# Two GRUs over a history on one Trainium2 core: sorted key rows written whole, sums moved to GpSimd, a count in bf16, results placed by one product

## The chip, the core and the metric

The kernel runs on one core of one Trainium2 chip. The metric is the device time of one launch in microseconds (us), as the median of several runs. Five engines work side by side: TensorE (PE, with its weight loads PEld), VectorE (DVE), ScalarE (ACT), GpSimd (POOL) and SyncE (SP), which here only issues DMA transfers. GpSimd issues the gathers (DMAs that fetch rows by a list of indices).

## The reference

A recommendation model (batch B = 1024, history of T = 100 steps, width H = 128). A GRU runs over the history and gives a key per step; an attention MLP scores each key against the item; the masked softmax of the scores pools the keys. The first 100 columns of the pooled array, transposed, are then the attention weights of a second recurrence (AUGRU) over the same keys. A final MLP reads the AUGRU's state at each row's own length.

```python
_, gru_seq = jax.lax.scan(gru_step, h0, jnp.swapaxes(item_historical_embedding, 0, 1))
keys = jnp.swapaxes(gru_seq, 0, 1)
feat = jnp.concatenate([keys, q, keys - q, q * keys], axis=-1)
score = _mlp(feat, [(att_W0, att_b0), (att_W1, att_b1), (att_W2, att_b2)], jax.nn.relu)
score = jnp.where(mask[:, :, None] == 1, score, -jnp.inf)
attn = jax.nn.softmax(score, axis=1)[..., 0]
pooled = jnp.einsum('bt,btd->bd', attn, keys)
att_seq = pooled.T[:T]
def augru_step(h, inp):
    x_t, a_t = inp
    ti = jnp.concatenate([h, x_t], axis=-1)
    r = jax.nn.sigmoid(ti @ aug_Wr.T + aug_br)
    u = jax.nn.sigmoid(ti @ aug_Wu.T + aug_bu)
    h_hat = jnp.tanh(jnp.concatenate([h * r, x_t], axis=-1) @ aug_Wh.T + aug_bh)
    u = a_t[:, None] * u
    h_new = (1.0 - u) * h + u * h_hat
    return (h_new, h_new)
...
attention_feature = jnp.take_along_axis(aug_out, sequential_length - 1, axis=1)
comb = jnp.concatenate([user_embedding, item_embedding, hist_sum, item_embedding * hist_sum, attention_feature], axis=1)
scores = _mlp(comb, [...], jax.nn.sigmoid)
```

`hist_sum` is the masked sum of the history divided by the length. The AUGRU needs a row only up to its length.

## The kernel before

The batch is two halves of 512 rows; the 128 hidden values lie on the partitions, the rows of a half along the free dimension. Instructions are written in the order in which each engine runs them (a manual schedule), so a transfer that waits on SP holds up every transfer written after it on SP, and likewise on each engine.

**First phase (`gru_phase`).** Steps s = 0 to 99 for both halves. PE multiplies (L588), ACT and DVE do the gates, the attention MLP of a step follows one step later (L770). Its scores, one row per half and step, go by a small DMA on SP into `s_b` (L825). After a group of steps DVE transposes `s_b` (L865), the softmax is carried on, and the pooled sums are updated with pairs of operations (L699 the product, L700 the sum, L689 the rescaling of the old sum), on GpSimd or DVE. Keys are collected in `kt` tiles, and every four steps `store` (L669) writes them to DRAM (`keys_d`) on SP, for later. Besides, a bf16 mask `m` is loaded per step and GpSimd sums the history (L573, L574). At step 8 a count of the rows still alive at each step (`count`, L354) is made on PE: a product of the 0/1 table `alive` with `ones`. It says which of three tables of widths the second phase may take (`over_d`).

**The tail of the first phase**, after the loop: attention of the last steps, the last softmax, the pooled sums of the remaining keys. The sums of the columns that are needed first (`soon`, 64 values a partition) come before those of the others (`rest`, 448 values). Of the first, `first_w` (L1114), PE's `by_row` and `first` and DVE's L1136 and L1137 make the AUGRU's first state `h_all`. Then the pooled array is written to DRAM (`pooled_d`, 8 DMAs on SP, L1146) and the last keys are stored (L669).

**Second phase (`augru_phase`).** Steps t = 1 to 99. The batch is sorted by length, so the width of a step shrinks (510, 506, 500, ...). `half_step` does one half: L1264 (the key's part of the three gates), L1268 (the state's part), ACT L1276, L1292, L1293, DVE L1298 to L1308. It needs the keys in sorted order, which indirect DMAs on POOL fetch from `keys_d` (`load_row`, L193); from step 12 on each is held back by a one-column copy (L192) from the product `rest` of L1308. PE and DVE transpose them (L1246, L1253). The attention weights are gathered from `pooled_d` into `att_r`, transposed (L1213), written to `att_d` and loaded to all partitions by SP as `at` (L1200, L1216, L1228), used in L1305. Late steps are done for both halves at once. Rows whose state is final go through the last MLP in blocks of 128 (`predict`); the very last block is placed by L1496 into the array of all results, which holds them 32 times over the partitions.

Keys are stored in groups. READ is the number of steps in a gathered group: 4, then 8 for each. So the keys of steps 4 to 11 are one group of `keys_d`, in 128 x 256 pieces, 32 gathers of 128 KB in all: 4 on POOL at the last GRU step but one, 4 behind the loop (L193), 8 behind the sums of half 0 and 16 in the second phase.

Of the kernel before, what the change touches and what calls it, by code (L numbers as in the profile page):

```python
# [9 lines left out]
F32 = mybir.dt.float32  # L10
# [42 lines left out]
WHOLE = 1  # L53
READ = [G] * WHOLE + [2 * G] * ((T - WHOLE * G) // (2 * G))
READ += [T - sum(READ)] * (sum(READ) < T)
# [30 lines left out]
def kernel(ctx: ExitStack, tc: tile.TileContext, a: dict, out: bass.AP):  # L86
# [31 lines left out]
        dram.tile([B, n * P] if q < WHOLE else [NK * P, n * R], F32, name=f"keys_d{q}")  # L118
        for q, n in enumerate(READ)
    ]  # L120
    mask_d = dram.tile([T, B], BF16, name="mask_d")
    inv_d = dram.tile([B, 3], I32, name="inv_d")
# [22 lines left out]
    used_s = const.tile([P, NH, GH, T - SOON], U8, name="used_s")  # L145
    all_y = pooled.rearrange("p k r -> p (k r)")[:, :BQ]
    idx_p = const.tile([P, HB // PR], I32, name="idx_p")
# [19 lines left out]
    def load_rows(q, i, width, tiles):  # L167

        n = READ[q]
        if q < WHOLE:  # L170
            r = rows[q, i] = tiles.tile([P, GH, n * P], F32, tag="once", name="rows")
            for g in range(GH):
                gather(r[:, g, :], keys_d[q], g, i)
                yield
            return

        parts, tag = (2, "kt") if tiles is kx else (1, "rows")
        some = [
            tiles.tile([P, KH // parts, n * R], F32, tag=tag, name="rows") for _ in range(parts)
        ]  # L180
        rows[q, i] = some
        for k in range(-(-width // R)):
            load_row(q, i, k)
            yield

    def load_row(q, i, k):
        some = rows[q, i]
        part, at = divmod(k, KH // len(some))
        r = some[part]
        if later.get("pace") is not None:  # L190

            nc.gpsimd.tensor_copy(r[:, at, 0:1], later["pace"])  # L192
        nc.gpsimd.indirect_dma_start(  # L193
            out=r[:, at, :],
            out_offset=None,
            in_=keys_d[q],
            in_offset=bass.IndirectOffsetOnAxis(ap=idx_k[:, k, i : i + 1], axis=0),
        )
# [5 lines left out]
    def gru_phase(pools):  # L204
# [72 lines left out]
        def load_later():  # L277
# [57 lines left out]

            alive = mid.tile([P, NG, T], F32, name="alive", **once)
            nc.vector.tensor_tensor(
# [4 lines left out]
            )  # L342
            ones = pre.tile([P, 1], F32, name="ones")
            nc.gpsimd.memset(ones, 1.0)
# [194 lines left out]
        class Half:  # L539
# [127 lines left out]
            def store(self, q):  # L667
                row, part = divmod(q - WHOLE, 2)
                nc.sync.dma_start(  # L669
                    out=keys_d[WHOLE + row].rearrange("(k p) m -> p k m", p=P)[  # L670
                        :, self.ks, ts(part, G * R)
                    ],
                    in_=self.kt[q].rearrange("p k n c -> p k (n c)"),
                )
# [256 lines left out]
        early = [load_rows(0, i, HB, mid) for i in range(NH)]  # L931
        more_early = load_rows(1, 0, HB, kx)

        def gather_early(n):
            for _ in range(n):
                next(more_early)


        late, again, early_from = 6, 24, 84
        for s in range(T):  # L940
# [5 lines left out]
            def loads():  # L946
# [6 lines left out]
                if s == T - AHEAD:  # L953
# [50 lines left out]
            if s == T - 2:  # L1004
                gather_early(4)
            for half in halves:
# [21 lines left out]

        gather_early(4)
        some(0, 1)  # L1030
# [31 lines left out]
        exponents()  # L1062
        take(T + 1)
        some(4, 5)

# [84 lines left out]
        halves[0].store(q)  # L1150
        all_of(more_early)

    def augru_phase(pools, widths, alive):
# [260 lines left out]
        def predict(g, last=False):  # L1414
# [22 lines left out]
            if last:  # L1437
                p0 = [of_pool("p0")[:MC, :P] for _ in range(n)]
                for j in range(n):
                    nc.tensor.matmul(  # L1440
                        p0[j], lhsT=part[:, ts(j, MC)], rhs=ident, start=True, stop=False
                    )
                yield
                for j in range(n):
# [39 lines left out]
            nc.scalar.activation(f1, p1, AF.Sigmoid, bias=later["c1"])  # L1484
            yield
            p2 = of_pool("p2")[:, 0:1]
# [3 lines left out]
            nc.scalar.activation(y, p2, AF.Sigmoid, bias=later["c2"])  # L1490
            if not last:
                rows_of(early_d, y, True, None)
                return
            p = of_pool("po")[:, :BQ]
            for q in range(P // R):
                nc.tensor.matmul(  # L1496
                    p[ts(q, R), :],
                    lhsT=y.to_broadcast([P, R]),
                    rhs=later["places"][q // 2][:, ts(q % 2, BQ)],
                    start=True,  # L1500
                    stop=True,
                )
            nc.vector.tensor_add(all_y, p, all_y)

        def last_places():
            own = sp.tile([P, 1], F32, name="own3", bufs=1)
            nc.gpsimd.tensor_copy(own, idx_p[:, 0:1])
            later["places"] = []
            for i in range(NH):
                row = wp.tile([P, HB], F32, tag="att_r", name="places", bufs=2)  # L1510
                nc.gpsimd.iota(
                    row,
                    pattern=[[1, HB]],
                    base=i * HB,
                    channel_multiplier=0,
                    allow_small_or_imprecise_dtypes=True,
                )
                nc.gpsimd.tensor_scalar(row, row, own, None, ALU.is_equal)
                later["places"].append(row)

        def earlier_results():
            nc.sync.dma_start(
                out=all_y,
                in_=early_d.rearrange("(q c) o -> q (o c)", c=BQ)
                .unsqueeze(1)
                .to_broadcast([P // R, R, BQ]),
            )
# [4 lines left out]

        def spread(q):


            ahead = 3 if widths[FIRST[q]] > HB // 2 else 4
            n = NH * -(-widths[FIRST[q]] // R)
            return spread_over(n, NH * (FIRST[q] - FIRST[q - 1] + 1 - ahead))

# [8 lines left out]
        sorted_rows = [gather_weights(i) for i in range(NH)]  # L1548
        ahead = load_rows(1, 1, widths[FIRST[1]], kp)
        for _ in range(P // R):  # L1550
            next(ahead)
        due = spread_over(-(-widths[FIRST[1]] // R) - P // R, NH * (FIRST[1] - 2))
        jobs, final = [], None
        for t in range(1, T):
            if t == one:
                open_state(t - 1, 1)
                last_state(1)
            if t + 1 in FIRST[1:-1]:
                all_of(ahead)
                ahead, due = gathers(FIRST.index(t + 1) + 1), spread(FIRST.index(t + 1) + 1)  # L1560
            for i in range(NH):
# [60 lines left out]
    with none.Else():  # L1622
# [8 lines left out]
        out=out.rearrange("(q c) -> q c", c=BQ),  # L1631
        in_=all_y.rearrange("(q r) c -> q r c", r=R)[:, 0, :],
    )
# [66 lines left out]
```

## Time and profile before

| what | us |
|---|---|
| median of 3 runs | 1998.83 (1998.15 to 1998.97) |
| the profiled execution | 2015.4 |
| its span, on which all rows stand | 2013.5 |
| mean granted clock of PE | 0.995 |

A row of a timeline reads: start in us, duration, engine, line, operation, output<-input, shape, count, and in brackets how long the engine stood idle before and what released it. A row of waits reads: engine, tile and line <- releaser: us in total, times, longest. A row of windows gives a stretch, its length, the busy time of each engine with its number of instructions, PE's granted clock, the DMA engines' share and GB/s.

### The profile page before, as it was taken

What the parts mean: (1) busy time and instruction counts of PE and PEld (TensorE: products, weight loads), DVE (VectorE), ACT (ScalarE), POOL (GpSimd) and SP (SyncE); (2) the same over time, 40 slices, a digit from 0 to 9 for tenths busy, and PEclk for the clock granted to TensorE, in tenths of its full rate; (3) what the DMA queues carried; (4) which work ended last, traced back from release to release, by engine and by line L of the source; (5) the groups of instructions that cost most, each with busy time, mean ns of one, the idle gap of its engine ahead of it and who ended that gap; (6) DMA issues with size and microseconds to landing.
All of it is one profiled execution on the core that took longest, in us unless ns stands there. A gap on an engine that the chain in (4) does not pass through costs nothing.

```text
span 2013.5 us, 40927 instructions
## 1 busy us (share of the span) xinstructions
PE 1982.8 (98%) x15324; PEld 875.7 (43%) x15324; DVE 1674.2 (83%) x3036; ACT 940.4 (47%) x1689; POOL 1262.1 (63%) x1300
## 2 busy tenths in 40 slices
PE   9999999999999999999999999999699999999998
PEld 2333333333333333333333333334244556678997
DVE  7888998887888897888888898998477777888885
ACT  4445444444445454445445454455234444445553
POOL 0333939569796959495987767989553354445331
PEclk9999999999999999999999999999899999999999
DMA  4443333323334334333432333332443333333331
GB/s 124 98 117 100 98 107 107 105 84 90 107 115 108 108 117 122 109 115 105 126 101 80 99 107 92 107 107 83 126 136 93 95 110 98 94 104 95 81 81 35
DMA packets 244572, 205.59 MB, mean 102 GB/s; under 512 B 61811, under 2 KB 207068, under 8 KB 244364
## 3 DMA queue, kind: packets, MB, share of 16 engines
q1 hardware_dynamic: 231852, 170.31, 29.9%
q0 software_dynamic: 12224, 32.05, 5.7%
q8 instruction: 122, 2.00, 0.4%
q14 instruction: 86, 0.70, 0.1%
q10 hardware_dynamic: 288, 0.52, 0.1%
HBM read 146.75 MB, written 54.42 MB: 100 GB/s over the span
## 4 chain that ended last, share of the span: by engine, by line
PE 93%; DVE 2%; POOL 2%; another core or an unknown queue 1%; ACT 1%; issue 1%; DMA 0%; SPq 0%; DVEq 0%; ACTq 0%; POOLq 0%
PE ps L588 48%; PE pm L770 17%; PE ph L1268 4%; PE pr L1268 4%; PE pu L1268 4%; PE ph L1264 4%; PE pr L1264 4%; PE pu L1264 4%; POOL pooled L700 1%; PE last L737 1%; POOL kw L699 1%; PE pr L1359 0%; PE ph L1359 0%; POOL hist L574 0%
## 5 line engine op out<-in xcount | busy, mean ns | idle before, releaser
L588 PE MATMUL ps<-x,wih 128*32 128x512 f32 x4800 | 601.9, 592 | 0.0
L588 PE MATMUL ps<-hn,whh 128*32 128x512 f32 x4752 | 596.8, 592 | 0.0
L588 PEld LDWEIGHTS ps<-x,wih 128*32 128x32 f32 x4800 | 174.4, 110 | 342.6 <-issue 337.9
L588 PEld LDWEIGHTS ps<-hn,whh 128*32 128x32 f32 x4752 | 172.8, 110 | 339.1 <-issue 337.0
L600 ACT ACTIVATE r<-ps,brz 128x512 f32<-128x512 f32 x200 | 137.5, 687 | 381.9 <-PE ps L588 381.7
L573 POOL TENSOR_TENSOR xm<-x,m 128x512 f32<-128x512 f32 x200 | 233.5, 1168 | 66.9 <-DMA m<-mask_d 66.6
L574 POOL TENSOR_TENSOR hist<-hist,xm 128x512 f32<-128x512 f32 x200 | 257.7, 1288 | 15.7
L193 POOL DMA_INDIRECT rows<-keys_d,idx_k x218 | 211.9, 972 | 85.2 <-POOL rows L192 49.7
L700 POOL TENSOR_TENSOR pooled<-pooled,kw 128x512 f32<-128x512 f32 x192 | 245.0, 1276 | 15.0
L699 POOL TENSOR_TENSOR kw<-kt,e 128x512 f32<-128x512 f32 x192 | 206.3, 1074 | 69.0 <-DVE e L888 69.0
L621 ACT ACTIVATE ps<-ps,bih 128x512 f32<-128x512 f32 x198 | 131.1, 662 | 229.8 <-DVE ps L618 228.7
L770 PE MATMUL pm<-hn,wk 128*32 128x512 f32 x1200 | 214.9, 592 | 0.0
L770 PE MATMUL pm<-kq,wkq 128*32 128x512 f32 x1200 | 214.8, 592 | 0.0
L1276 ACT ACTIVATE c<-ph,bh 128x510 f32<-128x510 f32 (+57 forms) x174 | 88.1, 506 | 254.5 <-PE ph L1268 222.1
L608 DVE SCALAR_TENSOR_TENSOR u<-ps,bhh,r 128x512 f32<-128x512 f32 x198 | 147.5, 745 | 68.8 <-PE ps L588 66.6
L770 PE MATMUL pm<-mv,w 128*32 128x512 f32 (+1 forms) x808 | 194.9, 592 | 1.0 <-DVE e L869 1.0
L192 POOL COPY rows<-rest 128x1 f32<-128x1 f32 x186 | 34.9, 188 | 209.5 <-DVE rest L1308 205.5
L631 DVE TENSOR_TENSOR d<-hn,ps 128x512 f32<-128x512 f32 x198 | 136.1, 687 | 35.9 <-ACT ps L621 35.5
L618 DVE TENSOR_TENSOR ps<-ps,u 128x512 f32<-128x512 f32 x200 | 140.0, 700 | 25.2 <-remote 4.1
L632 DVE TENSOR_TENSOR d<-ps,d 128x512 f32<-128x512 f32 x198 | 136.9, 691 | 26.1 <-ACT ps L622 11.1
L642 ACT COPY hn<-ps 128x512 f32<-128x512 f32 x198 | 115.5, 583 | 91.6 <-DVE kq L637 89.9
L1298 DVE TENSOR_TENSOR pu<-pu,c 128x510 f32<-128x510 f32 (+57 forms) x173 | 81.8, 473 | 89.7 <-ACT c L1276 62.9
(271 smaller groups left out, 3141.3 us busy)
## 6 DMA issues: line engine op xcount, KB each, us to landing
x<-in_hist_x SPq DMA_DIRECT2D x210, 256.0 KB
keys_d<-kt SPq DMA_DIRECT2D x48, 1024.0 KB
m<-mask_d SPq DMA_DIRECT2D x200, 128.0 KB
rows<-keys_d,idx_k POOLq DMA_INDIRECT x218
s_b<-mv SPq DMA_DIRECT2D x200, 8.0 KB
keys_d<-kt SPq DMA_DIRECT2D x32, 64.0 KB
mask_i<-in_mask SPq DMA_DIRECT2D x8, 200.0 KB
part_d<-part SPq DMA_DIRECT2D x2, 400.0 KB
```

The lines of the kernel that those rows point to most:

```text
L193: nc.gpsimd.indirect_dma_start(out=r[:, at, :], out_offset=None, in_=keys_d[q], in_offset=bass.IndirectOffsetOnAxis(ap=idx_k[:, k, i : i + ...
L573: nc.gpsimd.tensor_mul(d, x, m)
L574: nc.gpsimd.tensor_add(acc, acc, d)
L588: nc.tensor.matmul(p[ts(q, R), :], lhsT=w[:, g, ts(q, R)], rhs=v, start=(j == 0), stop=(j == len(parts) - 1),)
L600: nc.scalar.activation(r, pr, AF.Sigmoid, bias=brz[:, 0:1])
L608: nc.vector.scalar_tensor_tensor(out=u, in0=ph, scalar=bhh[:, 2:3], in1=r, op0=ALU.add, op1=ALU.mult,)
L618: nc.vector.tensor_add(pi, pi, u)
L699: eng.tensor_mul(d, k, w)
L700: eng.tensor_add(acc, acc, d)
L770: nc.tensor.matmul(p[i][s, :], lhsT=w[:, s], rhs=v, start=start, stop=stop)
L1264: nc.tensor.matmul(p, lhsT=m[:, 1, :], rhs=k, start=True, stop=False)
L1268: nc.tensor.matmul(p, lhsT=m[:, 0, :], rhs=v, start=False, stop=True)
```

## The change

1. Keys of steps 4 to 11 go to DRAM as whole rows (`wide_d`, one row of 1024 values per batch row: eight steps of 128). `sort_rows` gathers them whole (128 rows of 4 KB, 512 KB a gather, four a half) and stores them in sorted order (`sorted_d`, two stores of 1 MB a half, on SP). `load_sorted` loads from there, four plain DMAs of 256 KB a half on SP: steps 4 to 7 before the branch, steps 8 to 11 at step 3. The READ groups are 4, 4, 4, then 8 each. From step 12 on the gathers are as before.
2. The last sums of half 1 (`halves[1].pool(T, ..., rest)`) run on GpSimd instead of DVE.
3. `alive` and `ones` are bf16.
4. The last block of results is placed by one product: the final MLP's last product is added onto a 128 x 4 table that is 0 where a row belongs in a quarter of the batch and -1e30 elsewhere, so the sigmoid leaves 0 there; one product with `places` puts them on 4 rows of 256. The earlier results are loaded as 4 x 256 instead of broadcast, and written out from there.

```diff
-READ = [G] * WHOLE + [2 * G] * ((T - WHOLE * G) // (2 * G))
+READ = [G] * WIDE + [2 * G] * ((T - WIDE * G) // (2 * G))
...
+    wide_d = dram.tile([B, wide * P], F32, name="wide_d")
+    sorted_d = [dram.tile([HB, wide * P], F32, name=f"sorted_d{i}") for i in range(NH)]
...
+    def sort_rows(i):
+        pair = GH // 2
+        for part in range(GH // pair):
+            t = kx.tile([P, pair, wide * P], F32, tag="kt", name="sort")
+            for g in range(pair):
+                gather(t[:, g, :], wide_d, part * pair + g, i)
+            yield
+            nc.sync.dma_start(
+                out=sorted_d[i][ts(part, pair * P), :].rearrange("(g p) m -> p g m", p=P),
+                in_=t,
+            )
+    def load_sorted(q, i, tile):
+        n = READ[q] * R
+        rows[q, i] = [tile]
+        for p in range(P // R):
+            nc.sync.dma_start(
+                out=tile[ts(p, R)],
+                in_=sorted_d[i].rearrange("(k r) (p m) -> p r k m", r=R, p=P // R)[p][
+                    :, :, ts(q - WHOLE, n)
+                ],
+            )
...
-            alive = mid.tile([P, NG, T], F32, name="alive", **once)
+            alive = mid.tile([P, NG, T], BF16, name="alive", **once)
-            ones = pre.tile([P, 1], F32, name="ones")
+            ones = pre.tile([P, 1], BF16, name="ones")
...
             def store(self, q):
+                if q < WIDE:
+                    to = wide_d[self.cols, :].rearrange("(k r) (p m) -> p r k m", r=R, p=P // R)
+                    for p in range(P // R):
+                        nc.sync.dma_start(
+                            out=to[p][:, :, ts(q - WHOLE, G * R)],
+                            in_=self.kt[q][ts(p, R)].rearrange("p k n c -> p k (n c)"),
+                        )
+                    return
...
                 if last:
+                    all_of(sort[0])
...
             if s == T - 2:
-                gather_early(4)
+                next(sort[0])
+                next(sort[0])
...
-        gather_early(4)
+        next(sort[1])
+        next(sort[1])
         some(0, 1)
...
         take(T + 1)
+        all_of(sort[1])
...
         for half in halves:
-            half.pool(T, nc.vector, rest)
+            half.pool(T, nc.gpsimd, rest)
...
         halves[0].store(q)
-        all_of(more_early)
+        for half in halves:
+            load_sorted(WHOLE, half.i, kx.tile([P, KH, G * R], F32, tag="kt", name="rows"))
...
+            if last:
+                nc.tensor.matmul(p2, lhsT=f1, rhs=later["m2"].to_broadcast([M1, B // BQ]),
+                    start=False, stop=True)
+                y = sp.tile([P, B // BQ], F32, name="y4", bufs=1)
+                nc.scalar.activation(y, p2, AF.Sigmoid, bias=later["c2"])
+                p = of_pool("po")[: B // BQ, :BQ]
+                nc.tensor.matmul(p, lhsT=y, rhs=later["places"], start=True, stop=True)
+                nc.vector.tensor_add(all_y, p, all_y)
+                return
...
-            p = of_pool("po")[:, :BQ]
-            for q in range(P // R):
-                nc.tensor.matmul(p[ts(q, R), :], lhsT=y.to_broadcast([P, R]),
-                    rhs=later["places"][q // 2][:, ts(q % 2, BQ)], start=True, stop=True)
-            nc.vector.tensor_add(all_y, p, all_y)
...
-        ahead = load_rows(1, 1, widths[FIRST[1]], kp)
-        for _ in range(P // R):
-            next(ahead)
-        due = spread_over(-(-widths[FIRST[1]] // R) - P // R, NH * (FIRST[1] - 2))
+        ahead, due = iter(()), []
...
+            if t + 1 == FIRST[WHOLE]:
+                for i in range(NH):
+                    tile = kp.tile([P, KH, G * R], F32, tag="rows", name="rows")
+                    load_sorted(WHOLE + 1, i, tile)
```

**SP in the tail.** The rows from the score transfers of step 97 to those of step 100 (one pair of `s_b` per step; `sorted_d_73` is half 0, `sorted_d_74` half 1, `q` a small table), before and after:

```order
691 L825 DMA s_b_149<-mv 4x1x512
692 L825 DMA s_b_151<-mv 4x1x512
693 L962 DMA q_153<-perm_d 32x2x512
694 L825 DMA s_b_145<-mv 4x1x512
695 L825 DMA s_b_147<-mv 4x1x512
696 L825 DMA s_b_145<-mv 4x1x512
697 L825 DMA s_b_147<-mv 4x1x512
698 L825 DMA s_b_149<-mv 4x1x512
699 L825 DMA s_b_151<-mv 4x1x512
```

```order
691 L196 DMA sorted_d_73<-sort 128x2x1024
692 L860 DMA s_b_151<-mv 4x1x512
693 L860 DMA s_b_153<-mv 4x1x512
694 L196 DMA sorted_d_73<-sort 128x2x1024
695 L994 DMA q_155<-perm_d 32x2x512
696 L196 DMA sorted_d_74<-sort 128x2x1024
697 L860 DMA s_b_147<-mv 4x1x512
698 L860 DMA s_b_149<-mv 4x1x512
699 L860 DMA s_b_147<-mv 4x1x512
700 L860 DMA s_b_149<-mv 4x1x512
701 L860 DMA s_b_151<-mv 4x1x512
702 L860 DMA s_b_153<-mv 4x1x512
```

The score transfers of step 98 (the second pair) and 99 (the third) now stand behind three stores of sorted rows, the last of them half 1's first.

**SP at the handover**, from the pooled array's stores to the second attention load (`at`) of half 1, before and after:

```order
704 L669 DMA keys_d_72<-kt 128x16x128
705 L1146 DMA pooled_d<-pooled 32x16x32 x8
706 L669 DMA keys_d_72<-kt 128x16x128
707 L1620 UNCONDITIONAL_BRANCH
708 L1623 COMPARE_AND_BRANCH
709 L1200 DMA att_d_78<-att_t 4x512
710 L1228 DMA at<-att_d_78 128x506
711 L1228 DMA at<-att_d_78 128x500
712 L1200 DMA att_d_79<-att_t 4x512
```

```order
708 L704 DMA keys_d_71<-kt 128x16x128
709 L1181 DMA pooled_d<-pooled 32x16x32 x8
710 L704 DMA keys_d_71<-kt 128x16x128
711 L206 DMA rows<-sorted_d_73 32x16x128 x4
712 L206 DMA rows<-sorted_d_74 32x16x128 x4
713 L1673 UNCONDITIONAL_BRANCH
714 L1676 COMPARE_AND_BRANCH
715 L1236 DMA att_d_80<-att_t 4x512
716 L1264 DMA at<-att_d_80 128x506
717 L1264 DMA at<-att_d_80 128x500
718 L1236 DMA att_d_81<-att_t 4x512
719 L1264 DMA at<-att_d_81 128x506
```

Eight loads of sorted rows, four a half, now stand between the last key store and the first write of the attention weights.

**POOL at the handover**, from the last sums of half 0 to the first gathers of the attention weights (`att_r`), before and after:

```order
866 L689 TENSOR_TENSOR pooled<-pooled,e 128x16x28
867 L699 TENSOR_TENSOR kw<-kt,e 128x16x28
868 L700 TENSOR_TENSOR pooled<-pooled,kw 128x16x28
869 L699 TENSOR_TENSOR kw<-kt,e 128x16x28
870 L700 TENSOR_TENSOR pooled<-pooled,kw 128x16x28
871 L193 DMA rows<-keys_d_61,idx_k 128x256 x8
872 L1619 TENSOR_LOAD over_d
873 L1620 UNCONDITIONAL_BRANCH
874 L1623 COMPARE_AND_BRANCH
875 L1696 ISA
876 L158 DMA att_r<-pooled_d,idx 128x128
```

```order
869 L734 TENSOR_TENSOR kw<-kt,e 128x16x28
870 L735 TENSOR_TENSOR pooled<-pooled,kw 128x16x28
871 L734 TENSOR_TENSOR kw<-kt,e 128x16x28
872 L735 TENSOR_TENSOR pooled<-pooled,kw 128x16x28
873 L724 TENSOR_TENSOR pooled<-pooled,e 128x16x28
874 L734 TENSOR_TENSOR kw<-kt,e 128x16x28
875 L735 TENSOR_TENSOR pooled<-pooled,kw 128x16x28
876 L734 TENSOR_TENSOR kw<-kt,e 128x16x28
877 L735 TENSOR_TENSOR pooled<-pooled,kw 128x16x28
878 L1672 TENSOR_LOAD over_d
879 L1673 UNCONDITIONAL_BRANCH
880 L1676 COMPARE_AND_BRANCH
```

Eight gathers ahead of the branch are gone, and seven sums of half 1 stand there.

More of the change, by code (lines that the diff above doesn't have):

```diff
@@ L175, in load_rows @@
             return
[L177 to L181, printed above, removed]
+        rows[q, i] = [tiles.tile([P, KH, n * R], F32, tag="rows", name="rows")]
         for k in range(-(-width // R)):
@@ L184, in load_rows @@
             yield
+    def sort_rows(i):
[19 more added lines that the diff above has]
+            )
     def load_row(q, i, k):
-        some = rows[q, i]
-        part, at = divmod(k, KH // len(some))
-        r = some[part]
+        r = rows[q, i][0]
         if later.get("pace") is not None:
-            nc.gpsimd.tensor_copy(r[:, at, 0:1], later["pace"])
+            nc.gpsimd.tensor_copy(r[:, k, 0:1], later["pace"])
         nc.gpsimd.indirect_dma_start(
-            out=r[:, at, :],
+            out=r[:, k, :],
             out_offset=None,
@@ L931, in gru_phase @@
         early = [load_rows(0, i, HB, mid) for i in range(NH)]
[L932 to L936, printed above, removed]
+        sort = [sort_rows(i) for i in range(NH)]
         late, again, early_from = 6, 24, 84
@@ L1442, in predict @@
                     )
+                p2 = of_pool("p2")[:, : B // BQ]
+                nc.tensor.matmul(p2, lhsT=ident, rhs=later["others"], start=True, stop=False)
                 yield
@@ L1485, in predict @@
             yield
+            if last:
+                nc.tensor.matmul(
+                    p2,
+                    lhsT=f1,
+                    rhs=later["m2"].to_broadcast([M1, B // BQ]),
+                    start=False,
+                    stop=True,
+                )
+                y = sp.tile([P, B // BQ], F32, name="y4", bufs=1)
[4 more added lines that the diff above has]
+                return
             p2 = of_pool("p2")[:, 0:1]
@@ L1490, in predict @@
             nc.scalar.activation(y, p2, AF.Sigmoid, bias=later["c2"])
-            if not last:
-                rows_of(early_d, y, True, None)
-                return
-            p = of_pool("po")[:, :BQ]
-            for q in range(P // R):
[L1496 to L1503, printed above, removed]
+            rows_of(early_d, y, True, None)
         def last_places():
```

66 lines of the change are left out of this document (43 added, 23 removed).

## The prediction

> **What bounds the kernel now.** I read the page first (busy shares, then the chain that ended last), then windows over the joint between the two phases, then the timelines there.
>
> ```profile
> span 2013.5 us, 40927 instructions
> PE 1982.8 (98%) x15324; PEld 875.7 (43%) x15324; DVE 1674.2 (83%) x3036; ACT 940.4 (47%) x1689; POOL 1262.1 (63%) x1300
> PE 93%; DVE 2%; POOL 2%; another core or an unknown queue 1%; ACT 1%; issue 1%; DMA 0%; SPq 0%; DVEq 0%; ACTq 0%; POOLq 0%
> ```
>
> PE is busy 98% and carries 93% of the chain, so an edit counts only where PE stops. The change hardly touches the two long loops. It touches the start (a count), the joint near 1380 to 1455, and the last 4 us. Windows there (columns: us, then busy time and count of PE, PEld, DVE, ACT, POOL, then PE's granted clock, DMA share, GB/s):
>
> ```profile
> 1380.00:1405.00 25.00, 24.70 (x138) 14.37 (x138) 21.97 (x67) 18.67 (x35) 21.76 (x23) 1.00 0.33 100
> 1430.00:1453.00 23.00, 10.35 (x27) 4.55 (x25) 4.04 (x8) 2.73 (x5) 14.71 (x16) 0.75 0.38 113
> 1453.00:1470.00 17.00, 16.57 (x37) 7.67 (x38) 14.07 (x25) 6.60 (x10) 5.83 (x10) 0.84 0.42 112
> ```
>
> The second is the only real hole: PE busy 10.35 of 23 us, with POOL's 16 gathers in it, the very ones removed. Is it in the timed runs? DVE's, PE's and ACT's rows:
>
> ```profile
> 1432.11 0.69 DVE L1308 SCALAR_TENSOR_TENSOR rest<-pu,h_all 128x506 f32<-128x506 f32 x1
> 1454.82 0.69 DVE L1308 SCALAR_TENSOR_TENSOR rest<-pu,h_all 128x506 f32<-128x506 f32 x1
> 1470.89 0.68 DVE L1308 SCALAR_TENSOR_TENSOR rest<-pu,h_all 128x496 f32<-128x496 f32 x1
> 1475.94 0.68 DVE L1308 SCALAR_TENSOR_TENSOR rest<-pu,h_all 128x496 f32<-128x496 f32 x1
> 1436.46 1.00 PE L1264 MATMUL ph<-k,wh 128*128 128x500 f32 x2
> 1447.14 2.04 PE L1264 MATMUL pu<-k,wu 128*128 128x500 f32 x2 [9.68 <-issue]
> 1448.97 1.06 PE L1213 MATMUL pw<-ident,att_r 128*96 128x128 f32 x4
> ACT k L1247 <- remote: 12.0, 1, 12.0
> ```
>
> L1308 comes once per half step: 1432.11 is step 2 of half 0, 1470.89 step 4 of half 0, four half steps on, and the next comes 5.05 later. At that pace the fourth would stand at 1452.3, so the hole costs 18.6; up to two groups like L1213 (1.06 each) are extra work in it, so 16.5 to 18.6. The profiled execution took 2015.4 against a median of 1998.83: 16.6 longer. So nearly all the hole belongs to the profiled execution alone. That fits its look: ACT's wait has no releaser in this program ("remote"), and PE went on to 1437.5 before it stopped. I work against the profiled times but leave the hole out: of it the timed runs hold 0 to 18.6 − 16.6 = 2.0.
>
> **The change, part by part.**
>
> *A. The gathers of steps 4 to 11.* 32 gathers of 128 KB go, 8 of 512 KB and four 1 MB stores come. In timed runs this can only give back what is left of the hole: 0 to 2.0. I take the middle, **−1.0**. The extra store transfers at steps 8 and 12 sit in the GRU loop, on SP alone; I cost them at nothing, covered by inputs that are loaded steps ahead, and if that cover fails PE waits for a load there, within my upper bound.
>
> *B. The last sums of half 1.* Seven 448-wide DVE operations move behind GpSimd's own sums.
>
> ```profile
> 1409.00 0.69 DVE L1137 TENSOR_TENSOR h_all<-first,s_b 128x512 f32<-128x512 f32 x1
> 1409.61 0.62 DVE L699 TENSOR_TENSOR last<-kt,last 128x448 f32<-128x448 f32 x1
> 1413.43 0.62 DVE L700 TENSOR_TENSOR pooled<-pooled,last 128x448 f32<-128x448 f32 x1
> 1413.45 1.12 PE L1264 MATMUL ph<-hist,wh 128*128 128x510 f32 x2 [1.48 <-DVE last L699]
> 1405.07 0.97 POOL L699 TENSOR_TENSOR kw<-kt,e 128x448 f32<-128x448 f32 x1
> 1406.12 1.14 POOL L700 TENSOR_TENSOR pooled<-pooled,kw 128x448 f32<-128x448 f32 x1
> ```
>
> DVE's seven run from 1409.61 to 1414.05, and PE waits 1.48 for one of the last. This wait goes: **−1.5** (0 if PE then waits for the first r instead). On GpSimd seven at 0.97 to 1.14 are 7.4 us, 1407.3 to 1414.7: 0.6 later than DVE's end, so half 1's pooled store and what is gathered from it start 0.6 later. I cost that at nothing; the attention rows that come of it are used only from step 3 on.
>
> *C. The sorted stores on SP's queue, in the tail.* The first sorted store of half 1 is written on SP ahead of the score transfers (s_b) of steps 98 and 99. It waits for two gathers, which stand on POOL where the old ones stood:
>
> ```profile
> 1380.08 0.99 POOL L193 DMA_INDIRECT rows<-keys_d,idx_k  x1
> 1381.38 0.94 POOL L193 DMA_INDIRECT rows<-keys_d,idx_k  x1 [0.30 <-issue]
> 1379.00 12.02 SPq L825 DMA_DIRECT2D s_b<-mv  x6
> 1393.32 1.11 SPq L825 DMA_DIRECT2D s_b<-mv  x2
> 1388.47 0.73 DVE L865 STREAM_TRANSPOSE last<-s_b 128x512 f32<-128x512 f32 x1
> 1395.12 0.73 DVE L865 STREAM_TRANSPOSE last<-s_b 128x512 f32<-128x512 f32 x1 [0.22 <-DMA s_b<-mv]
> 1402.02 1.05 DVE L1114 TENSOR_TENSOR first_w<-pooled,used 128x128 f32<-128x128 f32 x1 [0.45 <-POOL pooled L684]
> 779.00 3.70 SPq L669 DMA_DIRECT2D keys_d<-kt  x2
> 782.75 3.40 SPq L134 DMA_DIRECT2D wh<-in_wh  x1
> 780.00:784.00 4.00, 4.00 (x42) 1.32 (x38) 3.37 (x5) 1.32 (x2) 3.92 (x4) 1.00 0.99 311
> ```
>
> Two gathers now carry 1 MB. At the 311 GB/s of the last row that is 3.4 us: from 1381.4 to about 1385. Then the 1 MB store goes out, beside the next two gathers (another 1 MB): 2 MB together end at about 1391.7. An s_b that gets past the store lands where it did; one that stays behind it lands at about 1391.7. The SP rows at 779 show the second: a small load behind two 1 MB stores held SP for 3.40. DVE reads s_b at 1388.47, without slack: idle before the next L865 is 0.22, and DVE is busy 21.97 of the 25 us to 1405. So all that ends in h_all comes late by between 0 and 1391.7 + 1.2 (an s_b's own way: the first of the two issues from 1393.32 ends near 1393.9, and DVE has it at 1395.1) − 1388.5 = 4.4. I take **+3.0**, nearer the queueing row, since the store can end before the gathers that share the engines with it. PE is busy until by_row needs L1114, so PE then waits.
>
> [...]
>
> *F. The sorted rows on SP's queue, at the handover.* Eight loads (2 MB) come behind the last key store and ahead of att_d and of the at loads of step 2.
>
> ```profile
> 1416.12 0.49 SPq L669 DMA_DIRECT2D keys_d<-kt  x1
> 1422.59 0.26 SPq L1200 DMA_DIRECT2D att_d<-att_t  x1
> 1424.03 0.82 SPq L1228 DMA_DIRECT2D at<-att_d  x2
> 1431.39 0.68 DVE L1305 TENSOR_TENSOR pu<-pu,at 128x506 f32<-128x506 f32 x1
> ```
>
> Key store and rows are 3 MB: at 311 GB/s 10.1 us from 1416.1, so 1426.2, where att_d now leaves at 1422.6: 3.6 late. The at load of step 2 (250 KB) takes an estimated 2.0 from its issue's end, the 1.2 of an s_b and 0.8 at 311 GB/s: it lands at 1426.4 now, at 1430.0 then, and DVE uses it at 1431.39, 1.4 later. So it is hidden by a little; but att_d must land before at is issued, each behind what is left of the rows, and gathers share the engines: 0 to +3.5. I take **+1.2**, nearer the slack. The second set of eight loads, at step 3, I cost at nothing: the at loads behind it are used a step later, 10 us; without that cover, 3.4.
>
> *E and D. The count and the last result.*
>
> ```profile
> 118.57 1.45 PE L354 MATMUL count<-alive,ones 128*1 128x100 f32 x15
> 121.30 0.25 PE L354 MATMUL count<-alive,ones 128*1 128x100 f32 x1 [1.28 <-issue]
> 2008.73 0.64 PE L1496 MATMUL po<-places,y 128*32 128x256 f32 x8 [0.35 <-ACT y L1490]
> 2009.43 0.42 DVE L1503 TENSOR_TENSOR pooled<-po,pooled 128x256 f32<-128x256 f32 x1 [3.57 <-PE po L1496]
> ```
>
> Sixteen f32 passes (1.45 + 0.25 = 1.70) become eight passes: half, **−0.85**; with the 1.28 pause, if it is in timed runs too, −2.1; 0 if the eight weight loads now show. Four products of two passes (0.64) become one product of two, which cannot be shorter than one pass of some 0.25: **−0.15**, from 0 to −0.4.
>
> **Sum:** −1.0 − 1.5 + 3.0 + 1.2 − 0.85 − 0.15 = **+0.7**, on the median 1998.83: **1999.5**. ±0.2% (4.0 us: 1994.8 to 2002.8) is about what a measurement of this kernel can tell from no change.
>
> **Rivals.**
> 1. *Both queues hide.* s_b and at pass the large transfers, C and F near 0: −3.5, 1995.3; with A, E and D at their far ends −1.5 − 2.1 − 0.4 − 2.0 = −6.0, 1992.8. For it: s_b uses few of the engines. Against: 3.40 at 782.75.
> 2. *The hole is in the timed runs after all*, made by 16 gathers in a row, and the 16.6 are spread elsewhere: it goes whole, −16.6 and the sum, about 1983. Against: the two numbers agree within 2.
> 3. *Slower: SP's order at full price.* C 4.4 and F 3.5, the rest as in the sum: +4.4, **2003.2**. It decides if the first pair of gathers lands after about 1386, since SP then lets nothing past.
> 4. *The clock.* PE's 3 us stop by C is followed by a half clock. After the hole a pair of matmuls took 2.04 where it took 1.00, and 1453 to 1470 ran at 0.84, that is 17 × 0.16 = 2.7 lost. With the sum: +3.4; with C at 4.4: +4.8, 2002.2 to 2003.6. [...]
>
> **How the numbers follow.** The sum 0.34 (own range 1996 to 2003); rival 1 0.27; rival 2 0.11; rival 3 0.20; rival 4 0.08. Faster by over 0.2%: 0.17 of rival 1, rival 2, 0.02 of the sum: 0.30. Slower: 0.15 of rival 3, 0.06 of rival 4, 0.03 of the sum: 0.24. Same: 0.46. The range leaves out rival 2 and the far end of 3 and 4: 1992 to 2005.
>
> **What would show it.** A: no hole at step 2 to 3, and a profiled execution within a few us of the median. B: no PE wait for L699's successor near 1413; GpSimd busy to about 1415. C: DVE waiting 2 to 4.4 for s_b before the first pair of L865, PE waiting as long before by_row. F: DVE's pu·at of step 2 waiting for at. E: count under 0.9 us. I am wrong if the first L865 starts no later against the last GRU step (C nil), if at is waited for over 4 us, or if the profile gains 17 and the timed runs gain it too.

## The result and the profile after

The changed kernel takes 2010.80 us (median of six runs, 2008.89 to 2011.44) against 1998.49 (six runs, 1996.03 to 1998.97): ratio 1.006, 95% interval 1.0048 to 1.0072, so 12.3 us slower. The forecast was 1999.5, range 1992 to 2005. The profiled execution took 2010.61, as long as the others, and rows of it can be added up against the median.

The page first: its span, and the chain that ended last.

```profile
span 2008.8 us, 40915 instructions
PE 95%; DVE 2%; DMA 1%; ACT 1%; issue 1%; DVEq 0%; ACTq 0%; SPq 0%
```

DMA now stands in the chain, and "another core or an unknown queue" is gone. Windows (us, then busy time and count of PE, PEld, DVE, ACT, POOL, then granted clock, DMA share, GB/s):

```profile
1392.00:1404.00 12.00, 9.72 (x35) 6.31 (x34) 8.36 (x29) 3.88 (x9) 6.95 (x7) 0.72 0.40 152
1430.00:1440.00 10.00, 9.34 (x28) 4.01 (x27) 1.98 (x3) 3.68 (x6) 4.10 (x5) 1.00 1.17 196
1440.00:1460.00 20.00, 17.68 (x45) 7.97 (x44) 14.50 (x24) 6.01 (x10) 3.68 (x7) 0.91 0.51 128
1460.00:1490.00 30.00, 25.62 (x59) 11.48 (x58) 18.46 (x30) 9.82 (x15) 13.79 (x23) 0.94 0.74 182
```

The one hole from 1430 to 1453 is gone, and three smaller ones have come, each with a lower granted clock. The first is the tail (timelines of POOL, SP, DVE and PE; in brackets the idle time ahead and what ended it):

```profile
1381.75 0.97 POOL L164 DMA_INDIRECT sort<-wide_d,idx  x1
1388.40 0.36 SPq L196 DMA_DIRECT2D sorted_d<-sort  x1
1388.85 6.88 SPq L860 DMA_DIRECT2D s_b<-mv  x6
1394.12 0.73 DVE L900 STREAM_TRANSPOSE last<-s_b 128x512 f32<-128x512 f32 x1 [3.96 <-DMA s_b<-mv]
1388.93 1.91 PE L805 MATMUL pm<-mv,w 128*32 128x512 f32 x8
1394.67 3.91 PE L805 MATMUL pm<-mv,w 64*32 64x512 f32 x8 [2.27 <-ACT mv L855]
1416.90 0.69 DVE L1172 TENSOR_TENSOR h_all<-first,s_b 128x512 f32<-128x512 f32 x1
1419.71 1.02 PE L1300 MATMUL ph<-hist,wh 128*128 128x510 f32 x2
```

The store of half 1's first sorted rows leaves at 1388.40 only, when its two gathers from 1381.75 on have landed; the score transfers follow it, and DVE, ready at 1390.16, waits 3.96. Then PE stops for 2.27 and its clock halves: the eight matmuls behind it take 3.91, where those of the half ahead took 1.91, and the same eight of 64 rows took 1.91 in the kernel before:

```profile
1390.65 1.91 PE L770 MATMUL pm<-mv,w 64*32 64x512 f32 x8
```

The second and third holes are at the handover:

```profile
1423.86 8.69 SPq L206 DMA_DIRECT2D rows<-sorted_d  x8
1432.75 1.37 SPq L1236 DMA_DIRECT2D att_d<-att_t  x1
1441.29 0.82 SPq L1264 DMA_DIRECT2D at<-att_d  x2
1444.53 0.69 DVE L1341 TENSOR_TENSOR pu<-pu,at 128x506 f32<-128x506 f32 x1 [6.86 <-DMA at<-att_d]
1447.64 2.05 PE L1304 MATMUL ph<-r,wh 128*128 128x506 f32 x2 [0.31 <-DVE r L1336]
1453.30 7.47 SPq L206 DMA_DIRECT2D rows<-sorted_d  x8
1460.87 2.75 SPq L1252 DMA_DIRECT2D att_d<-att_t  x1
1470.86 43.65 SPq L1264 DMA_DIRECT2D at<-att_d  x15
1474.33 0.68 DVE L1341 TENSOR_TENSOR pu<-pu,at 128x496 f32<-128x496 f32 x1 [6.05 <-DMA at<-att_d]
1476.47 1.09 PE L1300 MATMUL pr<-k,wr 128*128 128x492 f32 x2 [4.38 <-DVE k L1289]
```

Both times the attention weights' write (att_d) is issued behind eight loads of sorted rows, and the at load that must wait for it is issued 8.5 and 10.0 us later (1432.75 to 1441.29, 1460.87 to 1470.86). DVE waits 6.86 and 6.05 for at. In the trace's completion records the 256 KB loads land some 1.6 us apart, the first at 1429.6 and the eighth at 1440.9: about 162 GB/s, half the 311 that the prediction took from a key store.

### The profile page after: what moved, and what is told of

Same layout as the page of the kernel before. It is cut to its first block, busy times and chain, and to the rows that moved or that the text cites. A ratio compares the mean times of both kernels' runs of the same rounds, so it can differ in the third digit from the quotient of the medians.

```text
span 2008.8 us, 40915 instructions
## 1 busy us (share of the span) xinstructions
PE 1985.7 (99%) x15312; PEld 985.2 (49%) x15312; DVE 1668.2 (83%) x3021; ACT 941.5 (47%) x1689; POOL 1248.8 (62%) x1290
## 4 chain that ended last, share of the span: by engine, by line
PE 95%; DVE 2%; DMA 1%; ACT 1%; issue 1%; DVEq 0%; ACTq 0%; SPq 0%
PE ps L613 50%; PE pm L805 17%; PE ph L1304 4%; PE pu L1300 4%; PE ph L1300 4%; PE pr L1300 4%; PE pr L1304 4%; PE pu L1304 4%; DMA att_d<-att_t 1%; PE last L772 1%; PE pr L1395 0%; DMA at<-att_d 0%; PE ph L1395 0%; DMA s_b<-mv 0%; DVE ps L658 0%
## 5 line engine op out<-in xcount | busy, mean ns | idle before, releaser
L613 PE MATMUL ps<-x,wih 128*32 128x512 f32 x4800 | 782.7, 593 | 0.6 <-issue 0.6
L613 PE MATMUL ps<-hn,whh 128*32 128x512 f32 x4752 | 776.4, 592 | 0.0
L613 PEld LDWEIGHTS ps<-x,wih 128*32 128x32 f32 x4800 | 250.0, 110 | 304.2 <-issue 292.4
L613 PEld LDWEIGHTS ps<-hn,whh 128*32 128x32 f32 x4752 | 248.1, 110 | 297.7 <-issue 294.6
L805 PE MATMUL pm<-hn,wk 128*32 128x512 f32 x1200 | 259.7, 592 | 0.0
L805 PE MATMUL pm<-kq,wkq 128*32 128x512 f32 x1200 | 259.6, 592 | 0.0
L735 POOL TENSOR_TENSOR pooled<-pooled,kw 128x512 f32<-128x512 f32 (+1 forms) x195 | 249.6, 1280 | 15.3
L734 POOL TENSOR_TENSOR kw<-kt,e 128x512 f32<-128x512 f32 (+1 forms) x195 | 209.4, 1074 | 68.0 <-DVE e L923 67.9
L805 PE MATMUL pm<-mv,w 128*32 128x512 f32 (+1 forms) x808 | 242.2, 596 | 4.6 <-ACT mv L855 2.3
L218 POOL DMA_INDIRECT rows<-keys_d,idx_k x186 | 181.5, 976 | 75.7 <-POOL rows L217 70.6
L657 DVE TENSOR_TENSOR d<-ps,d 128x512 f32<-128x512 f32 x198 | 137.0, 692 | 31.9 <-ACT ps L647 17.8
```

Of the source, the lines that this page charges most:

```text
L218: nc.gpsimd.indirect_dma_start(out=r[:, k, :], out_offset=None, in_=keys_d[q], in_offset=bass.IndirectOffsetOnAxis(ap=idx_k[:, k, i : i + ...
L613: nc.tensor.matmul(p[ts(q, R), :], lhsT=w[:, g, ts(q, R)], rhs=v, start=(j == 0), stop=(j == len(parts) - 1),)
L734: eng.tensor_mul(d, k, w)
L735: eng.tensor_add(acc, acc, d)
L805: nc.tensor.matmul(p[i][s, :], lhsT=w[:, s], rhs=v, start=start, stop=stop)
```

## The experiments

The explanation to be tested, Q: transfers on SP's queue that stand behind the sorted rows wait until these have landed, at three places, and that is the loss. Times of one paragraph are from one chip unless it says otherwise; the chips differ, as the last experiments show.

**The first eight loads moved ahead.**

```diff
         all_of(sort[1])
+        for half in halves:
+            load_sorted(WHOLE, half.i, kx.tile(...))
...
         halves[0].store(q)
-        for half in halves:
-            load_sorted(WHOLE, half.i, kx.tile(...))
```

> The changed kernel, with the eight loads of sorted rows of steps 4 to 7 written on SP right behind the last sorted store, ahead of the pooled array's stores, instead of ahead of the attention weights (att_d, at). Nothing else moves. Theory Q (order on SP's queue: what stands behind the rows waits until they have landed): the wait of DVE's pu for at in step 2 (6.86 us) goes, PE's stop and half clock at 1440 to 1460 with it, worth 4 to 5 us: 2006 to 2007 against 2010.8. Rival L (load on the DMA engines: the added megabytes slow the small transfers wherever they stand on the queue): under 1.5 us. Rival G (the last sums of half 1 on GpSimd make the attention weights late): no change.

2005.45 (2004.92 to 2007.15); the changed kernel took 2010.8 on the chip of the result, 2012.4 and 2013.4 on two others, so 5 to 8 us faster, at or above what Q said; the sums of half 1 stay on GpSimd here, so G is out. Waits of DVE for DMAs from 1376 to 1500 (engine, tile, line <- releaser: us in total, times, longest), of the changed kernel and then of this one:

```profile
DVE pu L1341 <- DMA at<-att_d: 13.1, 3, 6.9
DVE last L900 <- DMA s_b<-mv: 4.8, 3, 4.0
```

```profile
DVE last L900 <- DMA s_b<-mv: 5.2, 2, 3.7
DVE pu L1341 <- DMA at<-att_d: 4.9, 1, 4.9
```

Of 13.1 us for at in three waits, one wait of 4.9 is left, that of the second set.

**The second eight, two a half step.** `load_parts` is `load_sorted` as a generator, one load at a time.

```diff
-                for i in range(NH):
-                    tile = kp.tile(...)
-                    load_sorted(WHOLE + 1, i, tile)
+                tiles = [kp.tile(...) for _ in range(NH)]
+                parts = [load_parts(WHOLE + 1, i, tiles[i]) for i in range(NH)]
+                parts = iter([p for ps_ in parts for p in (ps_,) * (P // R)])
...
+                for _ in range(2 if t in (3, 4) else 0):
+                    next(next(parts))
```

> The changed kernel, with the eight loads of steps 8 to 11 written two at a time behind each half step of steps 3 and 4, each pair ahead of one at load, instead of all eight at the start of step 3. Theory Q: the wait of 6.05 us for at near 1468 shrinks to under 1.5, PE's 4.38 idle and half clock near 1472 go, worth 5 to 6 us: 2005 to 2006. Rival L: the same megabytes in the same stretch, so under 1.5 us. Rival G: no change.

2004.60 (2003.12 to 2007.42): 6 to 9 us faster than the changed kernel (against the same three times), with one wait for at left, that of the first set. This is at or above what Q said.

```profile
DVE pu L1345 <- DMA at<-att_d: 7.3, 1, 7.3
```

The edit does two things at once: the loads come in pairs, and both att_d of these steps now leave ahead of the first pair (1449.10 and 1452.77, the pair at 1456.21). Which of the two does it was not taken apart.

**The stores behind the scores.**

```diff
             yield
-            nc.sync.dma_start(out=sorted_d[i]..., in_=t)
+            if i:
+                held.append((part, t))
+                continue
+            store_sorted(i, part, t)
+        for part, t in held if i else ():
+            store_sorted(i, part, t)
```

> The changed kernel, with both sorted stores of half 1 behind the last score transfers (the first one stood ahead of the score transfers of steps 98 to 100). The four gathers stay where they are. Theory Q: DVE's wait of 3.96 us for s_b goes, and with it PE's 2.27 stop and the half clock from 1394 to 1402; L1149 and what follows come 5 to 6 us earlier: 2004.8 to 2006. Rival L (gathers of 2 MB beside the score transfers): at least 2 us of the wait stays. Rival K (the clock falls for another reason): the wait goes, the half clock stays, worth 3 to 4.

2008.20 (2006.63 to 2010.70), 3 to 5 us faster: at or below what was expected. The window over the tail, of the changed kernel, and then this kernel's waits and its window:

```profile
1380.00:1406.00 26.00, 23.73 (x125) 14.57 (x125) 18.52 (x55) 15.12 (x30) 19.04 (x18) 0.87 0.50 181
```

```profile
DVE pu L1352 <- DMA at<-att_d: 14.2, 2, 8.5
DVE last L911 <- DMA s_b<-mv: 1.1, 1, 1.1
```

```profile
1380.00:1406.00 26.00, 25.32 (x131) 14.34 (x124) 21.57 (x65) 17.03 (x32) 22.26 (x24) 1.00 0.69 237
```

The wait for s_b is down to 1.1 and the granted clock of the tail is 1.00 instead of 0.87, so the half clock did come from that stop, against K. But the longest wait for at has grown from 6.9 to 8.5: part of the gain is handed to the next queue.

**All three.**

> The three moves together. Theory Q: they are worth 15 to 17 us, since they are in a row on the path: 1994 to 1996, below the 1998.5 of the kernel before, by the wait of PE for DVE's last sums (1.5), the count and the last result (about 1). Rival L: 2006 or more. If each move only hands its wait to the next transfer: between, 2000 to 2005.

> The three moves again, on one chip with the changed kernel. Theory Q: 14 to 17 us below the changed kernel, at 1995 to 1998, whichever chip it is. Rival: part of the first difference was the chip, and the gap is under 12.

> The three moves once more, as the mark for the kernel that is run beside it: 1995.5 to 1997.

> The changed kernel once more, on one chip with the kernel with the three moves and with the kernel before. So far the changed kernel took 2010.8 and 2012.4 on two chips, the kernel before 1998.5, 2013.5 and 2012.3 on three. If the stall of the kernel before is bound to the chip, this one tells again which of the two it is; the changed kernel itself takes 2010 to 2013 on each.

1996.87, 1995.83 and 1996.12 on three chips. On the second of them the changed kernel ran beside it: 2013.40 (2012.60 to 2015.13), 17.6 us more, a little above the 14 to 17 expected. Windows of the three moves (its second run):

```profile
1380.00:1405.00 25.00, 24.38 (x130) 14.16 (x122) 21.42 (x63) 17.00 (x32) 21.43 (x23) 1.00 0.79 230
1430.00:1453.00 23.00, 23.00 (x65) 11.07 (x64) 17.49 (x29) 8.72 (x14) 6.67 (x12) 1.00 0.49 117
1453.00:1470.00 17.00, 17.00 (x42) 7.79 (x41) 13.86 (x22) 7.36 (x12) 10.87 (x19) 1.00 1.11 252
```

PE runs through at full clock, while the DMA engines are busier than in the changed kernel (share 0.79 against 0.52 in the tail, 1.11 against 1.01 from 1453 to 1470). That rules out the load on the DMA engines, most plainly for the second set, which stays in its stretch: the same megabytes cost next to nothing in another place of the queue. In this kernel, too, the loads landed 1.4 us apart where nothing else moved, some 180 GB/s: with nothing beside them, too, they stayed well under 311. This version has the lowest median of all that ran.

The traces of the two kernels on that chip, laid side by side, tell where the 17.6 lie (us from one instruction's start to the other's; the spans are 17.8 apart):

| stretch | changed kernel | three moves | longer by |
|---|---|---|---|
| last gate r of the GRU to the last h_all | 44.72 | 38.74 | 5.98 |
| last h_all to the third gate product (ph<-hist,wh) | 2.79 | 3.04 | -0.25 |
| from there to rest of step 4, half 0 | 44.30 | 39.98 | 4.32 |
| from there to rest of step 5, half 1 | 22.15 | 14.96 | 7.19 |

**The sums of half 1 back on DVE**, in the kernel with the three moves (`half.pool(T, nc.vector, rest)`).

> The kernel with the three moves (1996.87), with the last seven sums of half 1 back on DVE. Theory S (prediction's step B): PE waits again for one of DVE's last sums ahead of the third gate product, 1.0 to 1.7 us slower than with the three moves: 1998 to 1998.5. Rival Z: first r of DVE is then the next to be late, so no change (within 0.5).

> The three moves with the last seven sums of half 1 back on DVE, on one chip with the three moves. Prediction's step B: 1.5 slower than these (1.0 to 2.0); in the first pair, on two chips, it was 2.1 (1999.0 against 1996.9).

In the first pair, on two chips, 1999.01 (1997.90 to 1999.98) against 1996.87; then 1999.01 (1997.92 to 2002.02) beside 1996.12 (1994.81 to 1996.54): 2.1 and 2.9 us in the medians, above what S said, and PE's wait is back (trace of the second):

```profile
1411.94 1.12 PE L1315 MATMUL ph<-hist,wh 128*128 128x510 f32 x2 [1.29 <-DVE last L749]
```

The trace shows 1.3 to 1.5 of it at this place (PE's rows of this kernel run 1.31 ahead of those of the three moves up to here, and 0.1 to 0.3 behind from here on). Some 2 us more lie behind step 5 (529.5 and 529.8 us from there to the end, against 527.4 to 528.2 in the three traces with the sums on GpSimd); what makes them was not found.

**The count and the last result alone**, put into the kernel before.

> The kernel before with edits 3 and 4 alone (the count in bf16, the last results placed by one product). Prediction's steps E and D: 1.0 us faster than the kernel before (0 to 2.5). Rival: the count's saving is lost in the pause of PE that follows it (1.48 us near 121 in the changed kernel), and only the 0.15 to 0.4 at the end is left.

2015.15 against 2016.74, ratio 0.9994 (0.9984 to 1.0004): not told from no change, so neither the 1.0 nor the rival is shown. In the changed kernel's trace the eight products of the count, and the product that places the last results, are:

```profile
L379 PE MATMUL count<-alive,ones x8: 205/207/209, 119.6 to 119.9; 128*1 128x100 bf16 x8
2004.25 0.59 PE L1535 MATMUL po<-places,y 128*4 128x256 f32 x2 [0.35 <-ACT y L1533]
```

**The hole of the kernel before.** In all these comparisons the kernel before did not take 1998.5 but 2013.45, 2012.31, 2016.74 and 2017.63, on four chips.

> The changed kernel as it is, once more, beside the kernel before and the next two. On the chip of the first four experiments the kernel before took 2013.45 (2009.0 to 2015.7), 15 us more than its 1998.5 elsewhere, and as much as its profiled execution (2015.4), which had the hole at 1430 to 1453. Theory H (the hole is a real stall of the kernel before that shows on some chips and in the profiled execution, and the changed kernel has none): the changed kernel takes 2010 to 2012 on either chip, so where the kernel before takes 2013 it is the faster one by 2 us. Rival P (the hole belongs to the recording, that chip is slower throughout): the changed kernel takes 2024 to 2027 there.

> The kernel before as it is, for a second trace. Theory H: where its time is 2010 or more, the trace has the hole of 16 to 19 us at step 2 to 3 of the AUGRU (DVE's pu waiting 10 us or more near 1433 to 1447); where it is 1999, there is none and the span is 1997. Rival P: the hole is there whatever the time is.

> The kernel before, run and traced once more, to see whether there is a chip on which its executions show no hole (1998.5 as in the comparison with the changed kernel) or whether every execution that leaves a trace shows it. Theory chip: sooner or later 1997 to 2000 with PE running through from 1430 to 1453. Theory trace: 2010 to 2017 again, with the hole.

The changed kernel took 2012.36 beside 2012.31 (ratio 1.000, 0.999 to 1.0009), and 2013.40 beside 2016.74 (0.9983, 0.9973 to 0.9992), where rival P had 2024 or more for it: these chips are not slower throughout. All three traces of the kernel before have the hole; none was had without it. Whether the six runs of 1998.5 lack it because of their chip or because they were not recorded stays open.

What makes it can be told in part. With twelve of the 16 gathers held back (`later["pace"] = rest[:, 0:1]` from step 1 on), without the 16 (a memset in their place), and with 8 of them:

> The kernel before, with twelve of the 16 gathers that POOL issued in a row from 1429.6 on held back by a one-column copy from the product rest, as all later gathers are: two to three a half step. The work is the same. Theory B (the row of 16 gathers makes the hole): the hole goes, 12 to 17 us faster than the kernel before where that takes 2013, and no change where it takes 1999. Rival N (the hole comes from elsewhere: the program's branch, the recording): no change on either.

> The kernel before without the 16 gathers of half 1's keys of steps 4 to 11 (those keys are zeros, set by one GpSimd instruction): it leaves out this part of the computation. Theory B (the row of gathers makes the hole; pacing them only halved it): on a chip where the kernel before takes 2012 or more, this takes 1996 to 1999 and PE runs through from 1430 to 1453. Rival N (the stall is of the start of the second phase, whatever POOL does): 2010 or more, with the hole.

> The kernel before with 8 of the 16 gathers of half 1's keys (the rest of those keys are zeros: it leaves out that part). Without any it took 2000.75 and had no hole, with all 2016.7. Theory of a build-up (records or descriptors of the gathers pile up until PE's semaphores wait): less than half of the hole stays, 2001 to 2005. Theory of one price a gather: 2007 to 2009.

They took 2010.20 (kernel before 2012.31; ratio 0.9987, 0.9977 to 0.9996), 2000.75 (2016.74) and 1997.20 (2017.63). The same window of the kernel before (its last trace), then of the three in this order:

```profile
1430.00:1453.00 23.00, 8.93 (x24) 4.09 (x24) 3.24 (x6) 2.57 (x4) 13.30 (x15) 0.67 0.32 96
```

```profile
1430.00:1453.00 23.00, 17.69 (x42) 7.94 (x41) 9.64 (x16) 4.45 (x7) 17.04 (x28) 0.78 0.36 111
```

```profile
1430.00:1453.00 23.00, 23.00 (x65) 10.97 (x64) 18.55 (x32) 8.52 (x13) 7.68 (x11) 1.00 0.40 120
```

```profile
1430.00:1453.00 23.00, 23.00 (x66) 10.91 (x65) 18.65 (x33) 8.52 (x13) 12.96 (x20) 1.00 0.52 159
```

With 8 gathers or none PE is busy all 23 us, with 16 it is 8.93, and the time falls by 20 and 16 us: the hole is the gathers' doing, and not at a price for each. Holding twelve of them back was worth 2 us instead of the 12 to 17 expected, and half of the hole stayed. It spread them less than was meant: POOL's rows there still show thirteen gathers from 1428.5 to 1445.2, 1.25 to 1.45 us apart, ahead of the first longer pause. How the gathers stop PE is not shown, and their number alone does not tell it. In the first trace of the kernel before, ACT's copy of the keys is late when only three of the 16 have been issued (1429.58 to 1432.08), right behind the eight of the attention weights:

```profile
1432.64 0.60 PE L1246 MATMUL pk<-ident,rows 128*128 128x128 f32 x4
1442.90 0.57 ACT L1247 COPY k<-pk 128x500 f32<-128x500 f32 x1 [11.95 <-remote]
```

The product ended at 1433.24, and the copy of it starts 9.66 later. In the run with 8 gathers a memset of 1.83 us stands between the two groups.

## Why the prediction was wrong

**The slower rival was the right one, and its sizes were too small.** Rival 3 (SP's order at full price) had 4.4 for C and 3.5 for F, 0.20 of the chances and 2003.2; the three places together were worth 17.6, where the sum had 4.2 for them.

- *F, the first loads, +1.2 of 0 to 3.5:* the step that failed first, and it measures some 4.3. The issue of att_d came no later than forecast: at 1432.75, 15.85 behind the last h_all, where 3.6 late would be 17.19 (1422.59 - 1409.00 + 3.6). What failed is its landing, on which the at load waits: 8.5 us from one issue to the other, where it was 1.44 (1422.59 to 1424.03). The key store's 311 GB/s was put on the loads of sorted rows, which ran at 162: 2 MB take 12.9 us instead of 6.7. The step did name that att_d must land before at is issued, but kept it within 3.5. The wait for at was 6.86.
- *F, the second set, 0:* "used a step later, 10 us" held for the at loads behind it, but not for att_d, which stands right behind the eight loads and whose landing the next at loads need. It cost a wait of 6.05, PE's stop of 4.38 and a slower clock (0.94 from 1460 to 1490), 7.2 in the table, where the step had 3.4 for a failing cover; moved, 6 to 9 us. The cover "a step later" was never checked against the slowest transfer that stands behind the loads.
- *C, +3.0 of 0 to 4.4:* it measures +6.2. POOL's first gather of the tail starts 1.67 later than before, DVE's last h_all 7.90 later (1409.00 to 1416.90). The queueing was right, with two sizes off. The first pair of gathers landed at 1388.4, where the forecast's 1385, moved by the same 1.67, is 1386.7; the second pair, issued from 1384.27 on, was under way beside it (landed by 1391.0). And the wait of 3.96 brought the half clock with it. Rival 4 had the clock, at 0.08.
- *B, -1.5:* right, in size and in mechanism. The difference between the two traces falls from 7.90 at h_all to 6.26 at the third gate product (1413.45 to 1419.71), 1.64. GpSimd's sums ended at 1421.3, 4.4 behind the last h_all, where DVE's had ended 5.05 behind it (1414.05), so what waits for them came no later.
- *E, -0.85:* PE's time for the count fell from 1.70 to 0.69 (0.48 and 0.21 in the timeline), -1.0 in the trace, but the pause beside it stays (1.28 before, 1.48 after), and no gain is left at the end of the GRU: its last gate r starts at 1368.64 to 1372.49 in the traces with the count in bf16, at 1368.82 to 1370.81 in the others. *D, -0.15:* from the first po product to the issue of out it was 1.15 and is 1.07, so -0.08.
- *A, -1.0, and "nearly all the hole belongs to the profiled execution alone":* in the deciding comparison A had next to nothing to give back, since the kernel before without a hole takes 1997.20 (with 8 of the gathers) to 2000.75 (without any), about its 1998.5 there. The second was argued from two numbers that agreed within 2 us, and it is not a fact about recording alone: on four chips the kernel before took 14 to 19 us more than its 1998.5. The 18.6 for the hole was a little high as well, for the four half steps that it counts at 5.05 each take 21.4 in the run with 8 gathers, which leaves 17.4. Rival 2 named the right cause, the row of 16 gathers, and on those chips leaving out 16 or 8 of them is worth 16 and 20 us, which is why the change is even or ahead there. Such a sum should have stood against both bases.

In sum, from the last gate r of the GRU to the end the changed kernel takes 636.3 us in the trace that goes with the result, and the kernel before with 8 gathers, which has no hole, 624.7. The 11.6 between them agree with the 12.3 measured. The kernel with the three moves takes 624.6 to 625.1, so the moves give back what SP's queue took, and not more: B's 1.6 is taken up by a tail that is still 0.5 to 1.4 longer up to the last h_all and an end that is 0.4 to 1.2 longer from step 5 on. It ran at 1996.12 beside the 1997.20 of the kernel before with 8 gathers, and 1.6 to 2.7 us below the 1998.5 of the kernel before, but on other chips; what these 1 to 3 us are is not shown.

SP's order held at all three places of the trace that goes with the result: the store of 1388.40 landed at 1393.6 and the score transfers behind it from 1393.7 on, the two sets of rows at 1440.9 and 1470.6 and the att_d behind them at 1441.2 and 1470.8. How long a stop of PE has to be for its clock to fall is not settled by the runs. In that trace the stop of 2.27 was enough (granted clock 0.50 from 1395.6 to 1402.3; the matmuls behind it took 3.91 instead of 1.91), and so was one of 2.01 at 1444.50 (0.50 from 1446.8 to 1450.1), while one of 1.48 at 121.00 left it at 1.00; in the second trace of the changed kernel one of 2.70 at 1444.30 left the granted clock of 1440 to 1460 at 1.00.

## What to carry to other kernels

A bulk transfer is not free because the data is needed late: list what is issued behind it on the same queue until it has landed, small writes whose landing another load waits for above all, and place it where nothing on the path stands behind it, or cut it into pieces between them (here the first eight loads moved ahead were worth 5 to 8 us, the second eight in pairs, with att_d ahead of them, 6 to 9). Take a transfer's rate from one of the same shape and direction (here 162 GB/s for the loads, where 311 had been taken from a store). A stall that only one execution shows is to be priced both ways, with it and without it, until it is known what makes it.

## What the runs showed of the hardware

Plain loads of 512-byte runs onto 32 partitions (256 KB each) ran at about 162 GB/s beside the gathers of the attention weights and at some 180 where nothing else moved, while 311 were moved in a stretch with two stores of 512-byte runs from 128 partitions (780 to 784 in the kernel before). Where a small write stood behind 2 MB of such loads on the same queue, the load that depends on it was issued 8.5 and 10.0 us behind the write; without such loads ahead it was 1.44. Leaving out the sixteen gathers of 128 KB at the start of the second phase made the kernel before 16 us faster, leaving out eight of them 20, on two chips. The same time was in its measured times on four chips, and not in the comparison that decided.
